# Two kept tiles of g for every unit, a ring of twelve, and a new slot layout in a sparse graph convolution

## The chip, the cores and the metric

One Trainium2 chip; the kernel uses one of its cores. The time is device microseconds of one execution, the median over several runs. Before the change: 1553.8 us, median of 3 runs (1552.07 to 1555.2). One execution was also profiled; it took 1553.88 us, of which the profile's span covers 1552.2 us.

## The reference

```python
HW = einsum('bnf,fo->bno', x, W)               # 8 x 4096 x 256, W is 256 x 256
A_norm = relu((A + A.T) * 0.5)                 # 4096 x 4096
D = sum(A_norm, axis=1)
d = D ** -0.5                                  # 0 where D is 0
out = relu(einsum('nm,bmo->bno', eye - d[:,None] * A_norm * d[None,:], HW))
y = layernorm(x + out, axis=-1)
```

A is an adjacency matrix with weights of 0.05 to 0.12. An entry (i, j) is there with a chance that falls with i and with j, so the first rows and columns (the hubs) are dense and the rest is sparse. The diagonal is always there. Everything is float32.

## The kernel before, in words

**First stage, to about 594 us.** A is symmetrised in 512 x 512 blocks and written to a DRAM tensor `a_dram`; the degrees give r = D^-0.5. In the same time g = r * (x W) is formed in row tiles of 128 x 2048 (8 batches times 256 outputs) and written to `g_dram`, 8192 bytes a row. The product of row tile 0 of the output, which is dense, is done there too (`lead`, L536).

**Second stage, from 594 us.** The other 31 row tiles are taken in 16 units: unit u holds row tiles 2u+1 and 2u+2, the last unit only one. The units run in the order `SEQ` (L24): 1 to 7, 0, 8 to 15. For a unit the kernel finds, on the chip, which rows of g it needs at all: those whose 256 columns of A_norm hold something. The first `HUBS[u]` row tiles of g are left out of this search: they are kept in SBUF over the whole stage (`hubs`, L865, loaded at L957), and are multiplied whole. All other rows are gathered.

A needed row is sorted by the 32-column strips that it touches. A row that touches one strip of the eight is of one of eight single kinds, and there are kinds of two strips, of one whole row tile, and one kind 0 for everything else (`KINDS`, L22). Each unit has a number of slots of 64 rows for each kind (`CAPS`), and the slots stand in an order (`FIRST`); two slots make a gathered tile of 128 rows. A row for which its kind has no slot left moves on to a wider kind, at last to kind 0. If kind 0 is full, a flag (`over`, L356) makes the kernel do all again densely at the end (L1211).

**The steps.** `steps_of` (L789) makes the list of TensorE steps of a unit, when the program is built, from CAPS, FIRST and HUBS alone. A whole step multiplies one tile (a kept hub or a gathered tile) with all 128 columns of one row tile: 4 banks of 512 columns. A round (L812) packs up to eight small products of 64 rows by 32 columns that lie on different parts of the array, taken from the first `REACH` = 5 tiles that still have some to do; it also goes over 4 banks. A float32 product is two instructions in the profile, so a whole step is 8 instructions on L1121 and a round of eight products 64.

**The ring.** Gathered tiles go into a ring of `RING` = 11 tiles (`gather`, L907). Each tile is two indirect DMAs on POOL's queue: L914 brings the weights from `a_dram` (128 x 128, or 128 x 256 for tiles that serve both row tiles), L922 the rows of g (128 x 2048; empty slots are skipped once the ring has been filled). `gather_ahead` (L932) is called after every step. Its rule is

```python
while eaten < asked and not uses_left[order[eaten]]:
    eaten += 1
while asked < len(order) and asked - eaten < RING:
    gather(asked)
    asked += 1
```

so slots come free in the order of asking: a tile still in use holds back all later ones.

**What else runs beside the steps.** The loop at L1131 places everything at a counted distance from the steps: `run_later(2)` after each step counts down what `after(n, ...)` has put off, so n is twice the number of steps. For each row tile there are the residual's load on ACT's queue (L725), the eviction on ACT (L731), the normalisation on VectorE (L741 to L774), and the store on SP's queue (L784), nine steps later. For each unit VectorE and TensorE make the index lists of a unit two to four places later (`prepare`, `lists`, L1049 and L1064). The rows of A for a hub are loaded on POOL (`load_hub_rows`, L895), 64 KB for each hub and row tile. An SP instruction after each bank of a round (L1188) keeps two rounds from writing one bank at a time.

Of the kernel before, what the change touches and what calls it, by code (L numbers as in the profile page):

```python
# [22 lines left out]

SEQ = [1, 2, 3, 4, 5, 6, 7, 0, *range(8, 16)]  # L24

HUBS = [2, 2, 2, 2, 3, 3, 2, 3, 3, 2, 3, 2, 3, 2, 3, 0]

CAPS = [
    [3, 4, 3, 3, 3, 2, 3, 3, 2, 3, 3, 3, 3, 3, 11],
    [3, 3, 3, 3, 3, 3, 3, 2, 3, 3, 2, 2, 2, 2, 6],  # L30
    [2, 3, 3, 3, 3, 3, 3, 3, 3, 2, 2, 2, 2, 2, 4],
    [3, 2, 3, 3, 2, 2, 2, 3, 3, 2, 2, 2, 2, 2, 3],
    [2, 2, 2, 3, 3, 3, 3, 3, 3, 2, 2, 2, 1, 1, 2],
    [2, 3, 3, 3, 3, 2, 3, 3, 3, 2, 1, 1, 1, 1, 2],
    [2, 2, 3, 3, 3, 2, 3, 3, 3, 2, 1, 1, 1, 1, 2],
    [2, 3, 3, 3, 3, 3, 3, 2, 2, 2, 1, 1, 1, 1, 1],
    [2, 2, 2, 3, 3, 2, 2, 3, 2, 2, 1, 1, 1, 1, 1],
    [2, 2, 2, 3, 3, 2, 2, 3, 3, 2, 1, 1, 1, 1, 1],
    [1, 3, 2, 3, 3, 2, 2, 3, 3, 1, 1, 1, 1, 1, 1],
    [1, 2, 3, 3, 3, 3, 3, 3, 3, 1, 1, 1, 1, 1, 1],  # L40
    [2, 2, 2, 2, 2, 2, 2, 2, 3, 1, 1, 1, 1, 1, 1],
    [2, 2, 2, 2, 2, 2, 2, 2, 2, 2, 1, 1, 1, 1, 1],
    [2, 2, 2, 2, 2, 2, 2, 2, 2, 1, 0, 0, 1, 1, 2],
    [3, 4, 4, 4, 4, 0, 0, 0, 0, 0, 0, 0, 0, 0, 0],
]

FIRST = [
    [0, 6, 10, 3, 13, 25, 19, 16, 27, 22, 44, 30, 47, 50, 33],
    [9, 0, 3, 6, 12, 18, 21, 16, 27, 24, 32, 30, 40, 42, 34],
    [3, 0, 5, 11, 8, 25, 19, 16, 22, 14, 34, 32, 38, 36, 28],  # L50
    [7, 2, 4, 10, 0, 24, 17, 19, 14, 22, 33, 26, 28, 35, 30],
    [0, 7, 5, 2, 9, 12, 23, 17, 20, 15, 31, 29, 26, 33, 27],
    [6, 8, 11, 0, 3, 22, 14, 17, 24, 20, 28, 33, 31, 32, 29],
    [0, 5, 7, 10, 2, 14, 16, 19, 24, 22, 32, 31, 33, 30, 28],
    [9, 6, 3, 0, 11, 17, 14, 22, 20, 24, 26, 28, 29, 30, 27],
    [2, 0, 10, 7, 4, 12, 19, 16, 21, 14, 24, 26, 28, 25, 27],
    [3, 10, 8, 5, 0, 22, 20, 12, 15, 18, 24, 26, 27, 28, 25],
    [0, 4, 7, 1, 9, 21, 19, 12, 16, 15, 26, 28, 24, 25, 27],
    [0, 10, 7, 1, 4, 15, 18, 12, 21, 24, 26, 28, 27, 30, 29],
    [0, 6, 8, 2, 4, 14, 10, 12, 16, 19, 24, 22, 20, 23, 21],  # L60
    [8, 2, 6, 4, 0, 10, 12, 14, 18, 16, 20, 22, 23, 24, 21],
    [0, 2, 4, 6, 8, 10, 12, 14, 16, 18, 20, 20, 20, 21, 22],
    [12, 15, 4, 0, 8, 20, 20, 20, 20, 20, 20, 20, 20, 20, 20],
]


# [1 line left out]
def kernel(  # L68
# [38 lines left out]
    QU = P // E  # L107
    NE = 2 * QU
    HOLD = 10
    RING = 11  # L110
    REACH = 5
    LATE = 18
    EPS = 1e-5
# [100 lines left out]
    def patterns(u):  # L214

        def t(shape, name, dtype=F32, **kw):
            return ipool.tile(shape, dtype, tag=name, name=f"{name}_{u}", **kw)
# [13 lines left out]
        nc.vector.tensor_tensor(diag, diag, own[:, :, :nb], ALU.max)  # L231
        if HUBS[u]:
            nc.vector.memset(used[:, :, : HUBS[u]], 0.0)
        several = t([P, NB], "several", bufs=1)
# [554 lines left out]
    def steps_of(u):  # L789
# [35 lines left out]
        def full(t, b):  # L825
            return [(t, None, b, None)]
# [9 lines left out]

        held = range(HUBS[u])
        out = [full(-1, 0)] if HUBS[u] else []
        starts = [full(t, 0) for t in whole[15]]
# [3 lines left out]
        if blocks(u) == 1:  # L843
            return out + [full(t, 0) for t in whole[0]]
        out += [full(-1, 1)] if HUBS[u] else []
        rows = [[full(t, 0), full(t, 1)] for t in whole[0]]
# [9 lines left out]
    with (  # L856
# [5 lines left out]
            gath.enter_context(tc.tile_pool(name=f"gath_{k}", bufs=1)).tile([P, G], F32, name=f"g{k}")  # L862
            for k in range(RING)
        ]
        hubs = [  # L865
            gath.enter_context(tc.tile_pool(name=f"hub_{h}", bufs=1)).tile([P, G], F32, name=f"g_hub{h}")
            for h in range(max(HUBS))
        ]
        ring_rows = [apool.tile([P, 2 * P], F32, tag=f"a{k}", name=f"ga{k}") for k in range(RING)]
        hub_rows = [  # L870
# [36 lines left out]
        def gather(n):  # L907

            u, t = order[n]
            both = t >= bounds[u][1]  # L910
            at, gt = ring_rows[n % RING], ring[n % RING]
            gi, ai = plan[u]
            with queue("pool"):
                nc.gpsimd.indirect_dma_start(  # L914
                    out=at if both else at[:, :P],
                    out_offset=None,
                    in_=a_pairs if both else a_rows,
                    in_offset=bass.IndirectOffsetOnAxis(ap=ai[:, t : t + 1], axis=0),
                    element_offset=P if both else 0,
                )  # L920
            with queue("pool"):
                nc.gpsimd.indirect_dma_start(  # L922
                    out=gt,
                    out_offset=None,
                    in_=g_dram,
                    in_offset=bass.IndirectOffsetOnAxis(ap=gi[:, t : t + 1], axis=0),
                    bounds_check=N if n < RING else N - 1,
                    oob_is_err=False,
                )
            got[u, t] = (at, gt, P if both else 0)  # L930

        def gather_ahead():  # L932
            nonlocal asked, eaten
# [4 lines that stand above are left out]
# [329 lines left out]
```

## Time and profile before

| what | value |
|---|---|
| time, median of 3 runs | 1553.8 us |
| profiled execution: time, and its span | 1553.88 us, 1552.2 us |
| first step of unit 1; first step of unit 15; last record of unit 15 | 594.2; 1504.4; 1525.5 us |
| busy: PE, DVE, POOL, ACT | 1428.7, 1040.1, 744.4, 364.0 us |
| DMA: moved, mean rate | 546.70 MB, 352 GB/s |
| q0 (POOL), q1 (SP), q10 (ACT): share of the 16 engines' span | 48.0%, 23.7%, 22.4% |

A line of groups gives the line, the engine, the operation, output<-input, the count, the busy time, the mean ns of one, and the idle time before it with what ended it. A line of waits says who waited for whom, for how long in total, how often, and the longest. A line of stretches gives the stretch, its length, then each engine's busy time with its number of instructions, the granted clock of TensorE, the mean busy share of the 16 DMA engines, and what they moved in GB/s. A line of the timeline has start, duration, engine, line, operation and, in brackets, the idle time before it and what ended that.

### The profile page before, as it was taken

Reading aid. Unit: us, or ns where it says so; the run is one execution under the profiler, and the core shown is the slowest. Engines: PE = TensorE matmul, PEld = TensorE weight load, DVE = VectorE, ACT = ScalarE, POOL = GpSimd, SP = SyncE. Lnnn points to the kernel's source line nnn. Section 1 sums busy time; section 2 is a strip of 40 time slices with the busy share of each in tenths; the row PEclk is TensorE's granted clock in tenths of the full one; section 3 lists DMA queues with packets and bytes.
Section 4 is the critical chain, followed back from the end, with each engine's and each line's share of the span. In section 5 each row is a group of like instructions: output and inputs, shape, how many; then the busy total and the mean of one; then the engine's idle time right before and its main releaser. Section 6 shows DMA issues by size and latency. Waiting matters only on the chain.

```text
span 1552.2 us, 29354 instructions
## 1 busy us (share of the span) xinstructions
PE 1428.7 (92%) x11008; PEld 766.6 (49%) x11008; DVE 1040.1 (67%) x3135; ACT 364.0 (23%) x462; POOL 744.4 (48%) x1271
## 2 busy tenths in 40 slices
PE   6999989898989987999999999799999898999992
PEld 5877867677867742333333433243343333334331
DVE  6676589979855645038659579499119978968554
ACT  3555544444544430010100100100010010011111
POOL 4012010011314226756675775767555776667751
PEclk9999999989999987999999999899999999999996
DMA  9999999999989998999998998999877999999994
GB/s 349 362 366 401 398 374 344 369 329 350 362 320 343 341 391 307 377 374 334 394 377 302 401 366 309 394 348 372 357 273 256 391 376 324 330 399 400 390 390 149
DMA packets 217749, 546.70 MB, mean 352 GB/s; under 512 B 19627, under 2 KB 107995, under 8 KB 183547
## 3 DMA queue, kind: packets, MB, share of 16 engines
q0 software_dynamic: 55216, 286.49, 48.0%
q1 hardware_dynamic: 93472, 126.89, 23.7%
q10 hardware_dynamic: 68912, 131.37, 22.4%
q8 instruction: 89, 1.46, 0.4%
q14 instruction: 60, 0.49, 0.1%
HBM read 442.89 MB, written 136.34 MB: 373 GB/s over the span
## 4 chain that ended last, share of the span: by engine, by line
PE 61%; DMA 16%; DVE 13%; issue 5%; POOL 3%; ACT 1%; SPq 0%; ACTq 0%; POOLq 0%; DVEq 0%
PE py L1121 40%; PE pg L578 9%; DMA g<-g_dram,gi 5%; PE lead L536 5%; DVE sym L472 4%; DMA out_dram<-xr 3%; PE xtr L567 3%; PE tr L468 3%; DMA xin<-in_x_dram 3%; DVE sums L479 3%; DMA a_dram<-sym 2%; POOL ga L914 1%; DMA ga<-a_dram,ai 1%; DMA xr<-in_x_dram 1%; ACT sym L476 1%
## 5 line engine op out<-in xcount | busy, mean ns | idle before, releaser
L1121 PE MATMUL py<-g,ga 64*32 64x512 f32 (+1 forms) x7024 | 614.6, 608 | 40.9 <-DMA g<-g_dram,gi 37.8
L1121 PEld LDWEIGHTS py<-g,ga 64*32 64x32 f32 (+1 forms) x7024 | 219.6, 112 | 420.7 <-issue 331.4
L914 POOL DMA_INDIRECT ga<-a_dram,ai x264 | 284.7, 1079 | 160.4 <-PE py L1121 86.2
L922 POOL DMA_INDIRECT g<-g_dram,gi x264 | 296.6, 1123 | 105.7 <-issue 64.0
L731 ACT ACTIVATE y<-py,minus_r 128x512 f32<-128x512 f32 x120 | 75.6, 687 | 836.1 <-PE py L1121 694.0
L1121 PE MATMUL py<-g_hub,gh 128*128 128x512 f32 x592 | 267.4, 599 | 1.7 <-DVE pos_k L210 1.7
L578 PE MATMUL pg<-w_sb,xt 128*128 128x256 f32 x1024 | 231.3, 384 | 5.8 <-ACT xt L568 4.0
L472 DVE TENSOR_TENSOR sym<-tr,adj 128x512 f32<-128x512 f32 x256 | 161.7, 682 | 78.0 <-PE tr L468 71.6
L578 PEld LDWEIGHTS pg<-w_sb,xt 128*128 128x128 f32 x1024 | 195.1, 193 | 34.1 <-ACT xt L568 4.4
L480 POOL TENSOR_SCALAR uses<-sums 128x64 uint8<-128x64 f32 x64 | 27.6, 431 | 350.6 <-DVE sums L479 312.2
L1121 PEld LDWEIGHTS py<-g_hub,gh 128*128 128x128 f32 x592 | 109.3, 190 | 154.8 <-issue 146.1
L479 DVE TENSOR_REDUCE sums<-sym 128x64 f32<-128x2048 f32 x64 | 145.4, 2278 | 54.4 <-ACT sym L476 54.4
L413 DVE COPY low<-lists 128x17 f32<-128x17 f32 (+7 forms) x14 | 2.4, 173 | 247.4 <-PE lists L401 247.4
L468 PE MATMUL tr<-ident,adj 128*128 128x128 f32 x1024 | 138.9, 285 | 29.8 <-DVE sym L472 16.9
L476 ACT ACTIVATE sym<-sym 128x2048 f32<-128x2048 f32 x64 | 122.8, 1918 | 126.5 <-DVE sym L472 126.5
L468 PEld LDWEIGHTS tr<-ident,adj 128*128 128x128 f32 x1024 | 118.4, 146 | 57.1 <-DVE sym L472 32.0
L741 DVE TENSOR_TENSOR xr<-xr,y 128x2048 f32<-128x2048 f32 x31 | 70.9, 2286 | 59.1 <-ACT y L731 29.3
L750 DVE BATCH_NORM_STATS2 stats<-xr 128x6 f32<-128x256 f32 x256 | 87.0, 412 | 1.1
L567 PE MATMUL xtr<-ident,xin 128*128 128x128 f32 x512 | 73.4, 294 | 14.5 <-DVE sym L472 12.8
L774 DVE TENSOR_SCALAR xr<-xr,mv,root 128x256 f32<-128x256 f32 x248 | 84.4, 411 | 0.6
L536 PE MATMUL lead<-gt,strip 128*128 128x512 f32 x176 | 83.5, 598 | 0.0
L568 ACT COPY xt<-xtr 128x512 f32<-128x512 f32 x128 | 67.8, 593 | 46.0 <-PE xtr L567 27.6
(152 smaller groups left out, 1041.3 us busy)
## 6 DMA issues: line engine op xcount, KB each, us to landing
adj<-in_adj_dram SPq DMA_DIRECT2D x64, 1024.0 KB, 10.2
a_dram<-sym ACTq DMA_DIRECT2D x64, 1024.0 KB, 9.9
out_dram<-xr SPq DMA_DIRECT2D x31, 1024.0 KB, 22.9
xr<-in_x_dram ACTq DMA_DIRECT2D x29, 1024.0 KB, 16.2
xin<-in_x_dram SPq DMA_DIRECT2D x44, 512.0 KB, 12.1
g_dram<-gt ACTq DMA_DIRECT2D x22, 1024.0 KB, 8.0
xin<-in_x_dram POOLq DMA_DIRECT2D x20, 512.0 KB
g_dram<-held ACTq DMA_DIRECT2D x10, 1024.0 KB, 11.9
```

The costliest lines, as they stand in the source:

```text
L468: ins = nc.tensor.transpose(pt[:, c * P : (c + 1) * P], tji[:, c, a * P : (a + 1) * P], ident)
L472: nc.vector.tensor_add(sym[:, a, :], pt, tij[:, a, :])
L476: nc.scalar.activation(sym, sym, AF.Relu, scale=0.5)
L479: nc.vector.tensor_reduce(sums, sym.rearrange("p a (c q) -> p a c q", q=E), AX.X, ALU.add)
L536: nc.tensor.matmul(lead[c], lhsT=strip, rhs=g[:, c * S : (c + 1) * S], start=not done, stop=len(done) == NB - 1, skip_group_check=True,)
L567: nc.tensor.transpose(pt[:, k, c, :], xin[b // H][:, b % H + k, c * P : (c + 1) * P], ident)
L578: ins = nc.tensor.matmul(pg[:, k * FO : (k + 1) * FO], lhsT=xt[:, b + k, c, :], rhs=w_sb[:, c, :], start=(c == 0), stop=(c == FC - 1),)
L750: nc.vector.bn_stats(stats[:, b, :], z[:, b, :])
L774: nc.vector.tensor_scalar(z[:, b, :], z[:, b, :], mv[:, b, 0:1], rstd[:, b : b + 1], ALU.subtract, ALU.mult,)
L914: nc.gpsimd.indirect_dma_start(out=at if both else at[:, :P], out_offset=None, in_=a_pairs if both else a_rows, in_offset=bass.IndirectOff ...
L922: nc.gpsimd.indirect_dma_start(out=gt, out_offset=None, in_=g_dram, in_offset=bass.IndirectOffsetOnAxis(ap=gi[:, t : t + 1], axis=0), boun ...
L1121: return nc.tensor.matmul(py[2 * u + 1 + b][c][cols, :], lhsT=at[ps, off + cols.start : off + cols.stop], rhs=gt[ps, c * S : (c + 1) * S], ...
```

## The change

All numbers in it are tables and one constant; no line of the program's logic differs. `HUBS` has 2 for every unit but the last (seven units had 3), so the third kept tile of g and its rows of A are gone. `RING` is 12. `CAPS` and `FIRST` are new.

```diff
-HUBS = [2, 2, 2, 2, 3, 3, 2, 3, 3, 2, 3, 2, 3, 2, 3, 0]
+HUBS = [*[2] * 15, 0]
 CAPS = [
     [3, 4, 3, 3, 3, 2, 3, 3, 2, 3, 3, 3, 3, 3, 11],
-    [3, 3, 3, 3, 3, 3, 3, 2, 3, 3, 2, 2, 2, 2, 6],
-    [2, 3, 3, 3, 3, 3, 3, 3, 3, 2, 2, 2, 2, 2, 4],
+    [3, 3, 3, 3, 3, 3, 3, 2, 2, 2, 2, 2, 3, 3, 6],
+    [3, 3, 3, 3, 2, 2, 2, 2, 3, 3, 2, 2, 2, 2, 4],
...
 FIRST = [
-    [0, 6, 10, 3, 13, 25, 19, 16, 27, 22, 44, 30, 47, 50, 33],
-    [9, 0, 3, 6, 12, 18, 21, 16, 27, 24, 32, 30, 40, 42, 34],
+    [9, 12, 0, 6, 3, 19, 16, 21, 24, 26, 44, 30, 47, 50, 33],
+    [12, 0, 3, 9, 6, 21, 18, 24, 16, 26, 28, 30, 41, 32, 35],
...
     HOLD = 10
-    RING = 11
+    RING = 12
```

What `steps_of` makes of the tables, before > after, and the rows that a unit gathers (counted on the reference's inputs by the kernel's rule: a row outside the kept tiles with an entry in the unit's columns):

| unit (in order) | steps | gathered tiles | rows gathered |
|---|---|---|---|
| 1 | 21 > 21 | 22 > 22 | 2599 |
| 2 | 18 > 18 | 20 > 19 | 2325 |
| 3 | 17 > 17 | 19 > 19 | 2128 |
| 4 | 16 > 15 | 17 > 18 | 1943 > 2046 |
| 5 | 16 > 15 | 17 > 17 | 1874 > 1972 |
| 6 | 14 > 14 | 17 > 17 | 1855 |
| 7 | 14 > 13 | 16 > 16 | 1773 > 1874 |
| 0 | 28 > 28 | 27 > 27 | 3000 |
| 8 | 14 > 12 | 15 > 17 | 1690 > 1778 |
| 9 | 12 > 12 | 15 > 16 | 1652 |
| 10 | 13 > 12 | 15 > 14 | 1584 > 1680 |
| 11 | 12 > 12 | 16 > 15 | 1594 |
| 12 | 13 > 11 | 13 > 15 | 1489 > 1569 |
| 13 | 11 > 11 | 13 > 13 | 1537 |
| 14 | 13 > 11 | 12 > 13 | 1429 > 1505 |
| 15 | 5 > 5 | 10 > 10 | 987 |
| sum | 237 > 227 | 264 > 268 | 29459 > 30101 |

Of the steps, 121 > 114 are whole and 116 > 113 are rounds. Of the tiles, 64 > 68 bring weights for both row tiles. In every unit kind 0 has room for the rows that come to it, before and after, so the dense fallback is not run. SBUF holds the same 14 tiles of 128 x 2048: 11 + 3 before, 12 + 2 after, and since the ring is laid out ahead of the hubs, its twelfth tile lies where hub 0 lay, and hubs 0 and 1 where hubs 1 and 2 lay.

## The prediction

> **What bounds the kernel now.** I read the page first: which engine and which queue is full.
>
> ```profile
> PE 1428.7 (92%) x11008; PEld 766.6 (49%) x11008; DVE 1040.1 (67%) x3135; ACT 364.0 (23%) x462; POOL 744.4 (48%) x1271
> ...
> DMA  9999999999989998999998998999877999999994
> ...
> q0 software_dynamic: 55216, 286.49, 48.0%
> q1 hardware_dynamic: 93472, 126.89, 23.7%
> q10 hardware_dynamic: 68912, 131.37, 22.4%
> ...
> PE py L1121 40%; PE pg L578 9%; DMA g<-g_dram,gi 5%; PE lead L536 5%; DVE sym L472 4%; DMA out_dram<-xr 3%; PE xtr L567 3%; PE tr L468 3%; DMA xin<-in_x_dram 3%; DVE sums L479 3%; DMA a_dram<-sym 2%; POOL ga L914 1%; DMA ga<-a_dram,ai 1%; DMA xr<-in_x_dram 1%; ACT sym L476 1%
> ```
>
> Two resources are nearly full at once: TensorE at 92%, and the DMA engines, whose three queues add up to 94.1%. So time saved on one of them counts only as far as the other allows. The change touches only the second stage (594.2 to 1525.5 us), so next I cut that into stretches, and looked within them for places where the DMA engines stand still.
>
> ```profile
> 689.40:1050.80 361.40, 349.71 (x3353) 137.54 (x3352) 271.97 (x1006) 30.67 (x49) 246.61 (x235) 0.98 0.96 356
> 1050.80:1159.80 109.00, 105.73 (x862) 39.32 (x861) 41.33 (x165) 4.85 (x8) 65.31 (x66) 0.97 0.90 344
> 1159.80:1504.40 344.60, 329.03 (x3099) 130.14 (x3098) 270.25 (x993) 34.99 (x57) 235.99 (x224) 0.98 0.95 357
> ...
> 690.00:730.00 40.00, 40.00 (x409) 14.94 (x415) 38.05 (x146) 2.42 (x4) 25.78 (x25) 1.00 0.87 305
> 830.00:850.00 20.00, 16.38 (x160) 5.98 (x162) 18.77 (x88) 0.00 (x0) 10.32 (x11) 0.95 0.67 234
> 950.00:970.00 20.00, 20.00 (x125) 7.52 (x124) 19.08 (x60) 0.00 (x0) 10.33 (x9) 1.00 0.69 228
> 1150.00:1190.00 40.00, 40.00 (x333) 16.68 (x333) 31.43 (x134) 4.37 (x7) 17.36 (x17) 1.00 0.60 208
> ```
>
> The first three are units 2 to 7, unit 0, units 8 to 14. The others are holes in the DMA: 5.2, 6.6, 6.2 and 16.0 us of nothing moving (length times one minus the DMA share). With 1.6 at 1020, 7.8 at 1120, 1.6 at 1240, 3.3 at 1280 and 3.8 at 1330, from the same view, the holes are 52 us. What makes them is seen on POOL and PE beside one of them:
>
> ```profile
> 833.48 0.58 POOL L902 DMA_DIRECT2D gh<-a_dram  x1 [1.72 <-PE py L1121]
> 836.92 0.55 POOL L902 DMA_DIRECT2D gh<-a_dram  x1 [2.85 <-PE py L1121]
> 840.44 0.98 POOL L914 DMA_INDIRECT ga<-a_dram,ai  x1 [2.97 <-PE py L1121]
> 841.73 1.04 POOL L922 DMA_INDIRECT g<-g_dram,gi  x1 [0.30 <-issue]
> ...
> 848.10 7.45 PE L1121 MATMUL py<-g,ga 64*32 64x512 f32 x94 [3.62 <-DMA g<-g_dram,gi]
> ...
> POOL ga L914 <- PE py L1121: 86.2, 77, 9.7
> PE py L1121 <- DMA g<-g_dram,gi: 37.8, 18, 6.5
> ```
>
> The ring is full, so POOL asks for no tile until TensorE has finished with the oldest (840.44). Then several are asked for at once, and TensorE itself waits for the one it needs next (to 848.10). Each hole in the DMA is paid back later as a TensorE wait.
>
> **What the Trainium skill says.** "DMA: Bandwidth & Descriptors", section "Issuing engines are not separate DMA queues": transfers issued by different engines run on the same 16 DMA engines and interleave. The trace agrees: the shares of three queues sum to 94.1%. The same page, "Anatomy of one DMA — SWDGE (gpsimd) path", puts a fixed 2 us on such a transfer; here a tile asked for at 841.73 freed TensorE at 848.10, 6.4 us, with others beside it. "Perfetto Trace Analysis", "Identifying the Most-Contended Engine": the same gap repeating on the engine that should be full can mean too few buffers for the next tile. The nine holes, with POOL waiting for TensorE, fit that.
>
> **The sum of the stage before.** I take step times from the starts of consecutive steps: a whole step is 3.53 us (two of them on a hub tile fill 7.03 us at 829.59), a full round 3.43 to 3.59. The index-list products stretch 14 steps by 1.24. So 237 x 3.53 + 14 x 1.24 = 854 of the 930.7 us between 594.2 and the last step's end at 1524.9; 77 us are waits, 19 of them at the first two steps, for the ring's first tiles.
>
> **The change, part by part.**
>
> *Steps on TensorE.* 237 to 227: 10 x 3.53 = 35.3 us less. If its waits stayed at 77 us the kernel would take 1518.6. They can't, since the DMA gets more to do.
>
> *Bytes.* 642 more gathered rows of 8192 bytes: +5.26 MB. One hub tile fewer: -1.05 MB. 14 fewer loads of 64 KB for the hubs' rows of A: -0.92 MB. Four more tiles, as four more of 128 KB: +0.52 MB. Sum +3.81 MB. POOL's queue moved 286.49 MB in 48.0% of 1552.2 us, 2.60 us per MB, so +9.9 us of DMA time. Nothing hides it where the engines are full, so it counts whole; were all of it to fall into holes, it would be nothing. I take 9.9. POOL's own issue work, 0.95 + 0.30 + 1.00 + 0.30 = 2.55 us a tile at its usual pace, grows by 10 us for four tiles and falls by 14 x 0.6 = 8.
>
> *The twelfth ring tile.* Before each hole one more tile can be asked for. A tile is on average 30101 / 268 = 112 rows, 0.92 MB, and 0.08 MB of weights: 2.6 us of transfer. A hole shrinks by that, or by its own size if less; the two at 1120 and 1150 lie in one stretch paced by TensorE (unit 0 and the start of 8), and gain once. So 6 x 2.6 + 2 x 1.6 = 18.8 us. Bounds: 0, if something else holds the asking back, and 18.8.
>
> *The new layout.* Fewer steps also bring the release of the oldest tile forward: one step fewer in units 4, 5, 7 and 10, two in 8, 12 and 14. What is left of the holes near these is 4.0 (830), 3.6 (950), 13 (1150). One step of 3.5 in the first two and two in the third could take up to 14 us; a layout that keeps a tile longer would take 0. To choose I walked the steps by the ring's rule and counted, for each tile, the steps between being asked for and first needed. Before, 39 tiles have four steps or fewer and 9 have two or fewer; after (with ring 12), 11 and 1. Stretches of two or more steps in which nothing is asked for: 32 before, 20 after. That says the layout doesn't undo the ring's gain, but the count includes the ring's part, so I take 5 of the 14.
>
> *The start.* The first gather was asked for at 593.33, behind three hub loads; now behind two. Hub 0 lies where hub 1 lay, whose load waited for `lead` until 587.78 and not 584.58. That is covered: TensorE is in `lead` until 594.18 and the load needs some 4 us. Uncovered it would cost up to 3.2. The 2.7 us of the missing hub are in the byte sum.
>
> *What stays.* Unit 0 has the same 28 steps (99 us of TensorE for 82 of transfers), unit 15 the same 5, and after the last step the same finish: 1524.9 to 1552.2.
>
> Sum: +9.9 - 18.8 - 5 = -13.9 us on the profiled execution's 1553.88, so **1540.0 us**. That execution lies 0.1 us from the median of the runs shown, so no correction is made. In TensorE's ledger: 818.7 us busy and about 98 us waiting, 21 more than before.
>
> **Rivals.**
>
> *The holes don't close, only the bytes count (slower).* Place: units 4 to 14. POOL needs 2.55 us to ask for a tile, the engines 2.6 us to bring it; after a drought POOL asks for six in a row, slowed to 1.9 us a piece when the queue is full, so an extra slot need not fill a hole. Then +9.9: 1563.8. It decides once the holes shrink by less than 9.9 of their 52 us. For it: POOL is as slow as the DMA. Against: at the start of a hole POOL is idle and waits for TensorE, 86.2 us in 77 waits. Between this and my case lies a partial gain. Chance 0.13 for ending slower.
>
> *VectorE becomes the bound.* In units 2 to 7 it is busy 271.97 / 6 = 45.3 us a unit. A unit of 12 steps is 12 x 3.53 + 1.24 = 43.6 us, and units 8 to 11 now have 12 each while index lists are still made. A unit's first step must wait till VectorE has read the counts: unit 12 shows 1.7 us of it (DVE pos_k L210). Four units at 1.7 give 7 us back: 1547. Against: transfers need about 51 us a unit there (unit 9: 13.5 MB of g and 1.3 MB of weights at 2.60, and four row tiles of 1.05 MB at the 2.90 us per MB of q1), more than VectorE's 45.3. Chance 0.15.
>
> *It does what the step count says.* TensorE bound, waits unchanged: 1518.6. It would need the DMA engines to do 9.9 us more in 35 less, that is nearly all of the 52 us of holes closed, though unit 0 alone keeps most of 24. Chance 0.04 for under 1528.
>
> *No change.* The gains and the bytes cancel, within 3 us (0.2%, about what a measurement of this kernel can tell from none): 0.05.
>
> **How the numbers follow.** The likeliest case, holes closing by 19 to 29 us, has 0.63: its own range is 1533 to 1547 and the forecast 1540. With VectorE (0.15) and the step count (0.04), and a rest of 0.82 between them, faster is 0.82, same 0.05, slower 0.13. The range for 8 in 10 reaches from 1530 (the byte cost at nothing for half, and most of the 14 us of the layout) to 1553 (gain and bytes all but cancel); about 0.06 lie below and 0.14 above.
>
> **What would show it.** On L1121 the hub matmuls fall from 592 to 480, those on gathered tiles go from 7024 to 7136 (838 small products and 54 whole steps, 8 each); L914 and L922 rise to 268, L902 falls to 60. Right: the DMA share of units 2 to 7 and 8 to 14 rises, the holes near 830 and 950 shrink to under 4 us, POOL's wait for PE falls well under 86 us, and PE's wait for g rises. Units 2 to 7 end some 8 us earlier than at 1050.8. Wrong: holes of the same size at new places, or PE's waits named DVE at the start of units 9 to 12.

## The result, and the profile after

The changed kernel takes 1529.47 us (median of 4 runs, 1526.87 to 1530.94) against 1554.5 us (1552.07 to 1556.66) for the kernel before. The ratio is 0.9838, with a 95% interval of 0.9817 to 0.9858: 25 us faster, where 13.9 were forecast. The direction was right. The time lies half a microsecond below the range of 1530 to 1553.

The profiled execution took 1529.14 us, of which 1527.3 are the span. The page of the changed kernel, the same lines as before:

```profile
PE 1390.9 (91%) x11008; PEld 753.8 (49%) x11008; DVE 1040.8 (68%) x3135; ACT 363.7 (24%) x462; POOL 739.9 (48%) x1264
...
DMA  9999999999989997998999999999978999999994
...
q0 software_dynamic: 55392, 290.44, 48.7%
q1 hardware_dynamic: 93472, 126.89, 24.2%
q10 hardware_dynamic: 68912, 131.37, 22.8%
...
PE py L1121 31%; DMA g<-g_dram,gi 9%; PE pg L578 9%; PE lead L536 5%; DMA a_dram<-sym 4%; DVE sym L472 3%; DMA out_dram<-xr 3%; PE tr L468 3%; DMA xin<-in_x_dram 3%; PE xtr L567 3%; DVE sums L479 2%; DMA ga<-a_dram,ai 2%; POOL ga L914 2%; DMA adj<-in_adj_dram 1%; DVE stats L750 1%
```

TensorE loses 37.8 us of busy time, close to the 35.3 of the ten steps. POOL's queue moved 3.95 MB more, yet the three queues together are busy for no longer: 95.7% of 1527.3 is 1461.6 us, where before 94.1% of 1552.2 was 1460.6. On the chain, the steps' share falls from 40% to 31% and the gathered tiles' transfers rise from 5% to 9%.

The stretches of the changed kernel: units 2 to 7, unit 0, units 8 to 14, then units 2 to 14 as one, and the places of two of the old holes (the second lies in unit 6, which now starts at 927.1 us and not at 937.2, so its place is ten us earlier).

```profile
688.00:1033.00 345.00, 336.73 (x3124) 131.59 (x3123) 270.58 (x1004) 30.04 (x48) 238.98 (x228) 1.00 0.98 374
1033.00:1145.30 112.30, 105.79 (x858) 39.67 (x857) 43.52 (x167) 5.17 (x8) 65.69 (x67) 0.95 0.91 348
1145.30:1474.70 329.40, 304.94 (x3195) 121.38 (x3194) 269.84 (x992) 34.89 (x56) 235.20 (x222) 0.97 0.99 373
687.90:1474.70 786.80, 747.56 (x7175) 292.71 (x7174) 584.03 (x2161) 70.09 (x112) 539.87 (x516) 0.98 0.97 370
830.00:850.00 20.00, 20.00 (x177) 7.44 (x184) 18.77 (x92) 0.00 (x0) 10.55 (x12) 1.00 0.92 330
940.00:960.00 20.00, 20.00 (x180) 7.24 (x164) 18.74 (x88) 0.00 (x0) 13.84 (x16) 1.00 0.90 339
```

Units 2 to 14 of the kernel before, in the same view:

```profile
689.40:1504.40 815.00, 784.47 (x7311) 307.01 (x7310) 583.55 (x2162) 70.52 (x113) 547.91 (x524) 0.98 0.94 355
```

The DMA share is rounded to a hundredth; summed over the packets of the trace, the DMA engines were busy for 770.0 us of these units and idle for 45.0 before, and busy for 765.0 and idle for 21.8 after. So 23 us of holes closed. The busy part fell a little, although the bytes in it rose: 355 GB/s over 815.0 us is 289 MB, 370 over 786.8 is 291 MB. The gain lies on both sides of unit 0. By step starts, units 2 to 7 took 361.4 us and take 344.0, units 8 to 14 took 344.6 and take 329.4. Unit 0 itself takes 4.4 us longer (109.0 and 113.4; it starts at 1031.9, a little before the 1033.00 of the stretch shown). Unit 15, which was to stay as it was, takes 26.2 us and not 21.1: TensorE stands still there for 3.9 us before a tile of g, where it stood 1.4.

Waits between 590 and 1505 us in the changed kernel (who waited for whom: total, times, longest):

```profile
ACT y L731 <- DMA out_dram<-xr: 71.3, 2, 40.6
POOL ga L914 <- PE py L1121: 69.8, 76, 7.1
...
PE py L1121 <- DMA g<-g_dram,gi: 34.3, 16, 5.0
...
PE lists L401 <- ACT y L731: 6.5, 1, 6.5
...
PE py L1121 <- DVE pos_k L210: 5.0, 3, 2.0
```

POOL waits 69.8 us for TensorE where it waited 86.2, and TensorE waits 34.3 us for g where it waited 37.8. By step starts, the stage (first step to the end of the last) fell from 931.3 to 907.3 us. With 227 steps of 3.53 us and 14 x 1.24 for the index lists, 88.7 us of it are beyond the bare steps, against 77.3 before.

Not all of this is waiting. TensorE stands still for 55.0 us of the stage, against 43.6 before; in the other 34 us, before and after, steps took longer than 3.53. Part of that is the granted clock. A line of the timeline and one of a stretch in it (TensorE alone), then the same form of product within that stretch and, for comparison, between 1340 and 1361 us at full clock (count, busy us, mean ns):

```profile
1369.15 8.79 PE L1121 MATMUL py<-g,ga 64*32 64x512 f32 x124 [2.61 <-DMA g<-g_dram,gi]
1369.70:1373.10 3.40, 3.40 (x46) 0.51 0.97 362
L1121 PE MATMUL py<-g,ga 64*32 64x512 f32 x40 | 4.4, 955 | 0.0
...
L1121 PE MATMUL py<-g,ga 64*32 64x512 f32 x120 | 7.3, 592 | 0.0
```

In the stage of the changed kernel the clock was granted at half in eight stretches of 3.4 to 17.1 us, 54.6 us in all, in which TensorE was busy for 39 us; before in six, 51.2 us in all and 33 busy. Each of the fourteen starts within 5 us after the beginning of a standstill of 2.0 to 6.5 us. So in these two traces a wait of TensorE often costs more than its own length. As an estimate, half of the 39 and 33 us, 20 and 17 us of the stage, are lost in this way.

The standstills that have grown are not those for g: TensorE waits for VectorE at the start of a unit (1.7 to 5.0 us), and once 6.5 us for an eviction on ACT (1.1 before).

### The profile page after: what moved, and what is told of

Its sections match the earlier page's. It is cut to its first block, busy times and chain, and to the rows that moved or that the text cites. A ratio compares the mean times of both kernels' runs of the same rounds, so it can differ in the third digit from the quotient of the medians.

```text
span 1527.3 us, 29344 instructions
## 1 busy us (share of the span) xinstructions
PE 1390.9 (91%) x11008; PEld 753.8 (49%) x11008; DVE 1040.8 (68%) x3135; ACT 363.7 (24%) x462; POOL 739.9 (48%) x1264
## 4 chain that ended last, share of the span: by engine, by line
PE 50%; DMA 23%; DVE 16%; issue 6%; POOL 3%; ACT 2%; SPq 0%; ACTq 0%; POOLq 0%; DVEq 0%
PE py L1121 31%; DMA g<-g_dram,gi 9%; PE pg L578 9%; PE lead L536 5%; DMA a_dram<-sym 4%; DVE sym L472 3%; DMA out_dram<-xr 3%; PE tr L468 3%; DMA xin<-in_x_dram 3%; PE xtr L567 3%; DVE sums L479 2%; DMA ga<-a_dram,ai 2%; POOL ga L914 2%; DMA adj<-in_adj_dram 1%; DVE stats L750 1%
## 5 line engine op out<-in xcount | busy, mean ns | idle before, releaser
L1121 PE MATMUL py<-g,ga 64*32 64x512 f32 (+1 forms) x7136 | 627.0, 608 | 41.3 <-DMA g<-g_dram,gi 34.3
L1121 PEld LDWEIGHTS py<-g,ga 64*32 64x32 f32 (+1 forms) x7136 | 229.2, 113 | 422.8 <-issue 333.8
L914 POOL DMA_INDIRECT ga<-a_dram,ai x268 | 285.6, 1066 | 139.7 <-PE py L1121 69.8
L1121 PE MATMUL py<-g_hub,gh 128*128 128x512 f32 x480 | 220.7, 601 | 5.0 <-DVE pos_k L210 5.0
L1121 PEld LDWEIGHTS py<-g_hub,gh 128*128 128x128 f32 x480 | 87.6, 190 | 132.7 <-issue 118.2
L380 DVE TENSOR_TENSOR hot<-iota_q,at 128x1024 bf16<-128x1024 f32 x64 | 74.4, 1217 | 7.2 <-DMA a_dram<-sym 7.2
## 6 DMA issues: line engine op xcount, KB each, us to landing
xr<-in_x_dram ACTq DMA_DIRECT2D x29, 1024.0 KB, 20.4
xin<-in_x_dram SPq DMA_DIRECT2D x44, 512.0 KB, 12.6
```

The source lines that it names most:

```text
L914: nc.gpsimd.indirect_dma_start(out=at if both else at[:, :P], out_offset=None, in_=a_pairs if both else a_rows, in_offset=bass.IndirectOff ...
L1121: return nc.tensor.matmul(py[2 * u + 1 + b][c][cols, :], lhsT=at[ps, off + cols.start : off + cols.stop], rhs=gt[ps, c * S : (c + 1) * S], ...
```

## The experiments

Two theories stood at the start. By the prediction's, the ring's twelfth tile closes the holes (18.8 us) and the bytes cost 2.60 us per MB. By another, the tables do it: fewer steps and another layout, with bytes that cost little where another engine sets the pace. A gain or loss in us below is the difference of two ratios times 1554; it lies within 2 us of the difference of the medians. The interval of one ratio reaches some 3 to 4 us to either side, so a difference of two kernels under about 5 us is not clear of its uncertainty.

### The ring alone, and the tables alone

The changed kernel with eleven ring tiles:

```diff
-    RING = 12
+    RING = 11
```

> The changed kernel with the ring back at 11 tiles; tables and hubs as changed. The sum of the prediction has 18.8 us for the twelfth tile: about 1548 us. If the missing 10 us came from the new tables and the fewer steps instead, the ring is worth less than was said and this stays near 1537 to 1542. If the ring gave more than 18.8, over 1550.

Measured: 1530.75 us, ratio 0.9851 (0.9825 to 0.9877). The twelfth tile is worth 2 us on top of the new tables, within what these runs can tell from nothing.

Next, only the seven units that lose their third hub get new rows of `CAPS` and `FIRST` (4, 5, 7, 8, 10, 12, 14); the other nine (the expectation below says eight) keep the old ones. Two hubs for all. One kernel has eleven ring tiles, the other twelve.

```diff
-HUBS = [2, 2, 2, 2, 3, 3, 2, 3, 3, 2, 3, 2, 3, 2, 3, 0]
+HUBS = [*[2] * 15, 0]
 CAPS = [
     [3, 4, 3, 3, 3, 2, 3, 3, 2, 3, 3, 3, 3, 3, 11],
     [3, 3, 3, 3, 3, 3, 3, 2, 3, 3, 2, 2, 2, 2, 6],
...
```

> Ring 11, two hubs everywhere, the new CAPS and FIRST only in the seven units that lost a hub; the other units have the old ones. So it holds all ten removed steps and most of the bytes, but neither the ring nor the new layout elsewhere. By the prediction's price of bytes (+9.9 less some 4 for steps): about 1560. If the bytes cost next to nothing and the ten steps count: 1535 to 1545.

> As the one before, with ring 12. Against the changed kernel only the layout of the eight units with unchanged hubs is undone. Walking the steps by the ring's rule, tiles with a lead of four steps or fewer are 19 here and 11 in the changed kernel (39 before). If leads as short as this are what makes the waits, some 3 to 6 us slower than the changed kernel, 1533 to 1536; if the layout of these units is worth nothing, 1529.

Measured: 1534.79 us with eleven tiles, ratio 0.9881 (0.9862 to 0.9899); 1526.6 with twelve, 0.9827 (0.9804 to 0.985). So most of the gain, 18.5 us, is there without a twelfth tile and without a new layout of the other nine units. A twelfth tile on top of this is worth 8.4 us, and the new layout of the nine other units nothing that shows (the whole change is at 0.9838), though it has fewer tiles with a short lead, 11 and not 19. No run has a twelfth tile with the old tables. Units 2 to 14 of the two kernels with eleven tiles, the mixed one first:

```profile
687.30:1482.30 795.00, 754.83 (x7216) 295.21 (x7215) 583.16 (x2160) 70.08 (x112) 554.26 (x521) 0.98 0.98 369
```

```profile
684.70:1477.80 793.10, 752.09 (x7176) 295.93 (x7175) 584.99 (x2161) 70.07 (x112) 553.23 (x520) 0.98 0.98 369
```

The DMA share is 0.98 in both, with the old ring: 18.4 and 19.1 us idle by the packets, against 45.0 before and 21.8 with twelve tiles. So the holes close without the twelfth tile. Nor are holes the same as time: with eleven tiles on the new tables the stretch is 6.3 us longer than with twelve, at less idle DMA, since the engines are busy for 774.0 us with the same tables' rows and not for 765.0. The page "Perfetto Trace Analysis" of the Trainium skill ("Optimization Strategy"), which the prediction followed, says that such gaps can mean too few buffers; here the step from eleven to twelve gave 2 to 8 us, not 19.

### What a megabyte costs

Both kernels with the gathered rows of the highest indices left out, so that 12.6 MB less is fetched in each. The steps stay as they are, and the output lacks these rows' part (the stale contents of the ring are multiplied in their place).

```diff
-    bounds_check=N if n < RING else N - 1,
+    bounds_check=N if n < RING else N - 257,
```

> The changed kernel, but the gather of g (L922) skips rows 3840 and above in every tile after the ring's first lap: some 1500 rows of 8 KB, 12.3 MB, are left out, with every instruction kept (it computes without these rows' products). If bytes cost what the prediction said, 2.60 us per MB: 32 us faster, 1497. If TensorE waits because tiles are asked for late, and not because the engines are full: no more than 5 to 12 us faster, 1517 to 1525.

> The kernel before, with the same rows left out of the gathers as in the changed kernel: some 1500 rows of g, 12.3 MB, with every instruction kept. In the changed kernel that gave about 7 us, 0.6 us per MB and not 2.60. If bytes count as little here, 4 to 9 us faster, 1545 to 1550. If the kernel before was held by the transfers and only the changed one is not: 20 to 32 us, 1522 to 1534.

Measured: 1522.26 us for the changed kernel, ratio 0.9795 (0.9763 to 0.9827), 6.7 us less than with all rows; 1545.8 for the one before, 0.9942 (0.9925 to 0.9959), 9.0 us less. That is 0.53 and 0.71 us per MB, and about 1.0 and 0.9 at the far end of the uncertainty. The prediction charged 2.60. Where the rest went is in the stretch over units 2 to 14 of the changed kernel with fewer rows:

```profile
685.80:1469.60 783.80, 746.33 (x7175) 295.06 (x7174) 586.06 (x2163) 70.50 (x113) 551.86 (x518) 0.98 0.96 359
```

Against 786.8 us at 0.97 and 370 GB/s, the engines move 10 MB less (359 x 783.8 is 281 MB; 370 x 786.8 is 291) and the stretch is 3 us shorter. By the packets, the engines are busy for 748.8 us and not 765.0, and idle for 35.1 and not 21.8. So 16 us of transfers were taken out, less than the 26 that 2.60 us per MB would give, and 13 of the 16 became idle DMA and not time. A share of 95% did not mean that the next byte costs a full share.

### What a step costs

The ten removed steps are put back into the changed kernel, with the same gathers. In the units that lost steps, hub 1 is multiplied once or twice more, so its part of the output is counted more than once.

```diff
+        held = [*held, *[1] * {4: 1, 5: 1, 7: 1, 8: 2, 10: 1, 12: 2, 14: 2}.get(u, 0)]
...
-        out += weave(rounds[:first_b1], [full(-1 - h, 0) for h in held[1:]], starts)
+        out += weave(rounds[:first_b1], [full(-1 - h, 0) for h in held[1:3]], starts)
...
-            [full(-1 - h, 1) for h in held[1:]],
+            [full(-1 - h, 1) for h in [1, *held[3:]] if HUBS[u]],
```

> The changed kernel, but the product of hub 1 is done once more in units 4, 5, 7 and 10 and twice more in 8, 12 and 14 (hub 1 counts double there): 237 steps as before, no byte and no gather more. If the removed steps are what made the kernel faster, some 19 us (what the mixed kernel with ring 11 gained) come back: 1545 to 1552. If the DMA engines set the pace, as the prediction had it, the steps fill waits and it stays under 1537.

Measured: 1595.51 us, ratio 1.0271 (1.0247 to 1.0294). This run doesn't measure steps. After the first product with hub 1, the next unit's rows of A were loaded into the same buffer, and the second product waited for that load, which the waits of this kernel name:

```profile
PE py L1122 <- DMA gh<-a_dram: 69.2, 8, 15.4
```

So the rows for the next unit were then loaded after the last use only:

```diff
-                if t < 0:
+                if t < 0 and not any((u, s) in steps[q + 1 : q + 40] for s in [step]):
```

> The experiment with the steps put back, mended: the earlier one loaded the next unit's rows of A over those that the doubled product still had to read, so that product waited for a load (77 us of TensorE waiting for gh<-a_dram) and its time says nothing on steps. Now the load follows the last use. 237 steps, the same bytes and gathers as the changed kernel (hub 1 counts double in seven units). If the removed steps made the kernel faster: 1543 to 1552. If transfers set the pace: under 1537.

Measured: 1533.83 us, ratio 0.9869 (0.9842 to 0.9896), 4.8 us above the changed kernel (the two intervals still overlap by a little). The prediction's third rival, that the step count sets the time, is refuted: this kernel has the 237 steps of the kernel before and is 20.4 us faster than it. The same count as above gives 57.5 us beyond the bare steps instead of 88.7, so thirty-one of the thirty-five microseconds of extra steps don't show in the stage. Eighteen of them go into standstills of TensorE (36.7 us instead of 55.0; for g 23.0 instead of 34.3, and the 6.5 for ACT are gone). The other thirteen come back because the steps take less long: the clock is at half for 30.7 us of the stage instead of 54.6, which by the same estimate (half of TensorE's busy time there, 21.7 us instead of 39.2) makes nine of the thirteen.

The other way, ten steps more are left out: the first product with hub 1, in all units but 1 to 5 (and the last, which has none), so that part of the output is missing. Nine loads of 64 KB fall away with them.

```diff
+        held = [h for h in held if not (h == 1 and u not in (1, 2, 3, 4, 5))]
```

> The changed kernel with the first product of hub 1 left out in the ten units from 6 on (one step of 3.53 us fewer in each, 35 us of TensorE; these products are missing from the result; nine loads of 64 KB fewer). If steps still count as ten of them did in the change (some 19 us for ten): 1508 to 1515. If units of 10 and 11 steps are too short for what runs at a counted distance beside them (stores, residual loads, lists) or for the transfers: within 8 us of the changed kernel, or slower.

Measured: 1520.75 us, ratio 0.9788 (0.9759 to 0.9817), 7.8 us less. A further step is worth 0.8 us of its 3.5: of the 35.3 us, 13.0 become standstill (68.0 us instead of 55.0), and 12.5 are lost because the other steps take longer, with the clock at half for 75.1 us of the stage instead of 54.6 (nine or ten of the 12.5 by the same estimate).

### VectorE as the bound

The changed kernel normalises one of the eight batches; the other seven are stored without their normalisation. That takes 71 us from VectorE.

```diff
-        for b in range(B):
+        for b in range(1):
```

> The changed kernel, but seven of the eight normalising instructions of a row tile (L774) are left out, except in the last one: 2.3 us less of VectorE for each of 31 row tiles, 71 us in all (those seven batches come out as x plus the product, not normalised). If VectorE were the bound of the 11 and 12 step units: 10 us or more faster, and the waits for DVE pos_k (5.0 us in 3) gone. If it only has that wait: 3 to 6 us. If TensorE or transfers set the pace everywhere: under 3 us.

Measured: 1522.1 us, ratio 0.9789 (0.9772 to 0.9806), 7.6 us less. VectorE is in the path, but no more than the others: 71 us less of it, 12.6 MB less for the DMA engines, or ten steps less of TensorE each give 7 to 8 us.

### The new wait on ACT

At unit 13 ACT stands still for 40.6 us before an eviction, and TensorE's list product waits 6.5 us for that eviction. ACT's own timeline in the changed kernel, then TensorE's:

```profile
1409.25 19.93 ACTq L725 DMA_DIRECT2D xr<-in_x_dram  x2
1429.28 2.42 ACT L731 ACTIVATE y<-py,minus_r 128x512 f32<-128x512 f32 x4 [40.55 <-DMA out_dram<-xr]
```

```profile
1430.02 1.00 PE L401 MATMUL lists<-val,hot 128*128 128x20 bf16 x32 [6.46 <-ACT y L731]
```

The residual's load (L725) goes into a buffer that an earlier store must have left. That load stands on ACT's queue and the eviction behind it. It may be that with shorter units a store that is put off nine steps comes later against the next load. If so, an earlier store should help. `LATE` is counted in half steps:

```diff
-    LATE = 18
+    LATE = 14
```

> The changed kernel with LATE = 14, stores two steps earlier than with 18. With 8 the stores stood on SP's queue waiting for VectorE (266 us), the bank turns queued behind them, and TensorE waited 181 us for SP. If VectorE is behind by two or three steps only now and then, the stores free the residuals' buffers 7 us earlier and the wait on ACT's queue at unit 13 shrinks: 1521 to 1527. If VectorE is behind by more than that in most units: slower, 1535 to 1560.

and the same with 8:

> The changed kernel with LATE = 8: a row tile is stored four steps after its normalisation and not nine. In the changed kernel the residual loads of unit 13 wait on ACT's queue for stores to free their buffers, and the evictions queue behind them (71 us of ACT waiting for out_dram<-xr in 2 waits, 6.5 us of the lists' products waiting for ACT), which no trace of before shows. If this is a new wait that the shorter units brought, some 5 to 10 us faster: 1520 to 1525, with that wait gone. If the wait is hidden, or the earlier stores hold back the gathers: 1529 or more.

Measured: 1575.21 us with 14, ratio 1.0143 (1.0117 to 1.0169); 1665.91 with 8, ratio 1.0724 (1.0701 to 1.0746). Both are far slower. The store is now issued before VectorE has finished, so SP stands at it. Two answers of the waits of the kernel with 8, SP's own and TensorE's:

```profile
SPq L784 <- DVE xr L774: 266.5, 20, 23.4
```

```profile
PE py L1121 <- SPq L1188: 180.8, 13, 19.7
```

In the changed kernel these are 13.8 and 3.5 us. Behind the store on SP stand the instructions that give the banks free between rounds (L1188), and TensorE waits for those. So the delay that makes the one wait on ACT keeps a much larger one off SP; whether that one wait costs the kernel anything was not settled, since no run takes it away alone.

### The start of the stage

With eleven ring tiles and two hubs, POOL's first requests come earlier than with twelve. POOL's timeline of the changed kernel, then of the changed kernel with eleven tiles:

```profile
587.41 0.55 POOL L957 DMA_DIRECT2D g_hub<-g_dram  x1 [16.43 <-PE lead L536]
588.09 1.08 POOL L902 DMA_DIRECT2D gh<-a_dram  x2
590.84 0.53 POOL L957 DMA_DIRECT2D g_hub<-g_dram  x1 [1.67 <-issue]
591.36 1.06 POOL L902 DMA_DIRECT2D gh<-a_dram  x2
592.72 1.05 POOL L914 DMA_INDIRECT ga<-a_dram,ai  x1 [0.30 <-issue]
```

```profile
586.29 0.55 POOL L957 DMA_DIRECT2D g_hub<-g_dram  x1 [13.42 <-PE lead L536]
...
591.37 1.05 POOL L914 DMA_INDIRECT ga<-a_dram,ai  x1 [0.30 <-issue]
```

The hubs lie where the `lead` product works until the first stage ends, and the gathers stand behind them on POOL. The experiment lays the hubs out ahead of the ring, which itself moves on by two tiles (three in the kernel before); no other line changes:

```diff
+        hubs = [...]
         ring = [...]
-        hubs = [...]
```

> The changed kernel with the hubs laid out ahead of the ring. With ring 12 the hubs lie one place further on, their loads wait for a later product of lead, and POOL's gathers queue behind them: the first gather is asked for 1.0 us before lead's end, as in the kernel before, and not 4.7 us before it as with ring 11 and two hubs. If that is what the twelfth tile cost at the start: the first gather 4 us or more earlier against lead's end, and the kernel 3 to 8 us faster, 1521 to 1527. If the first gathers then wait for places of their own, or the gain is lost in later waits: 1528 to 1531.

> The changed kernel with ring 11 and the hubs laid out ahead of the ring. Against the same with ring 12 (1519.4 us) it gives the worth of the twelfth tile without what it cost at the start. In the trace of ring 11 the first two steps waited 13.4 us and in that of ring 12 19.0, so of the 1.3 us measured some 5.6 were lost there: theory, ring 12 is worth about 7 and this runs at 1524 to 1529. If the twelfth tile is worth nothing by itself: 1518 to 1521. If the prediction's 18.8 holds and something else hid it: 1536 or more.

> The kernel before with the hubs laid out ahead of the ring and nothing else changed. In the changed kernel this gave 10 us. If the start's wait is passed on whole whatever the tables: 8 to 12 us faster, 1542 to 1546. If in the kernel before the time is given back at later waits, where the ring of 11 runs dry: under 5 us, 1549 to 1554.

Measured: 1519.41 us for the changed kernel so laid out, ratio 0.9785 (0.9759 to 0.981), 8.2 us less; 1521.05 with eleven tiles, 0.9794 (0.9778 to 0.9811); 1547.52 for the kernel before, 0.9966 (0.9952 to 0.9979), 5.3 us less. POOL's timeline of the first of these:

```profile
572.02 0.55 POOL L957 DMA_DIRECT2D g_hub<-g_dram  x1 [3.01 <-DMA g_dram<-held]
...
576.70 1.05 POOL L914 DMA_INDIRECT ga<-a_dram,ai  x1 [1.49 <-DMA a_dram<-diag]
```

The first gather is asked for 16 us earlier, at 576.70 and not at 592.72, and no longer behind a wait for `lead`. By step starts, unit 1's time beyond its bare steps falls from 19.0 to 6.9 us (it was 19.9 in the kernel before), and the stretch at half clock there from 17.1 to 3.4 us. Even with the start out of the way the twelfth tile is worth only 1.4 us (1521.05 to 1519.41) on the new tables.

Together with the mixed tables and twelve tiles, where the layout is worth 11.2 us:

> The mixed kernel with ring 12 (1526.6 us, 2.9 less than the changed kernel, within what was measured as uncertain) with the hubs laid out first: a candidate for the fastest. If the 10 us of the start and the 2.9 of the older layout add up: 1514 to 1518. If the layout's difference was chance: 1518 to 1521.

Measured: 1515.16 us, ratio 0.9755 (0.9732 to 0.9778). It is the fastest of all, 38 us below the kernel before and 13 below the change.

### What the third hub cost

What is left is to split the 18.5 us of the mixed tables with eleven tiles. First, the 1.05 MB load of a third hub is put back into that kernel, with its buffer (the same edit in the loop that makes the buffers and in the one that loads them); nothing uses it.

```diff
-        for h in range(max(HUBS)):
+        for h in range(3):
```

> The mixed kernel with ring 11 (1534.8 us), but the third hub is still loaded at the start, 1 MB ahead of the first gathers, and never used. It tells how much of the 18.5 us that the mixed kernel gained is the missing load at the start. First gather 3.7 us later against lead's end than in the mixed kernel, and 3 to 6 us slower: 1538 to 1541. If the start doesn't matter: 1535. If it is most of the gain: over 1545.

Measured: 1537.68 us, ratio 0.9903 (0.9885 to 0.9922), 3.4 us more, though the intervals overlap.

Then two kernels were to show the rest: the same load and the ten steps put back as above; and the old hubs in the steps, with the rows of the third hub gathered as well, so that they are multiplied twice.

> The mixed kernel with ring 11 and the third hub's load put back (1537.7 us), and the ten steps put back by doubling products of hub 1, with no byte more: 237 steps. In the changed kernel ten steps cost 4.8 us. If a step costs the same here: 1541 to 1545, and some 8 us of the mixed kernel's gain are due to the tables and to the 14 loads on POOL. If the ring of 11 makes steps dearer: 1548 or more, and nothing is left for the tables.

> The mixed kernel with ring 11, with all the third hub's work put back in its seven units: 14 steps, 14 loads of 64 KB on POOL and the 1 MB at the start, 241 steps in all, while the tables still gather the third hub's rows too (these count double). If the third hub's own work is what the mixed kernel got rid of: all of its 18.5 us come back and some more, 1551 to 1558. If the new tables of the seven units are themselves better for the waits: 1540 to 1548.

Measured: 1790.83 us, ratio 0.9971 (0.9954 to 0.9989), and 1804.12, ratio 1.0047 (1.0031 to 1.0062). These two ran on a chip on which the kernel before takes 1796.07 us (35 runs), and not 1552 to 1555 as in every other comparison. There, the waits of the first of them are led by one line:

```profile
PE py L1122 <- SPq L1189: 181.7, 81, 7.5
```

This is TensorE waiting for SP's turn of a bank (one line lower, since a line was added), 0.2 us in the profile of the kernel before and 3.5 us in the changed one. With another bound, the ratios can't be set against the rest, and the split stays open.

## Why the prediction was wrong

**Two terms of the sum failed, and their errors partly cancelled.** The first is the bytes: "Nothing hides it where the engines are full, so it counts whole", +9.9 us. At the measured 0.53 to 0.71 us per MB, 3.81 MB would cost 2.0 to 2.7 us (an estimate: these figures come from rows taken out of all units, not put in where the change put them), so the term was 7 to 8 us too dear. The reasoning behind it took the queue's busy time over its bytes for a fixed price. But the engines' busy time isn't fixed by the bytes: over units 2 to 14 it is 770.0 us for 289.1 MB before and 765.0 us for 291.2 MB after, summed over the packets, and the mean packet of 8 KB took 333 ns before and 328 after. And most of what is taken out leaves idle engines, not time.

The second is the twelfth ring tile, -18.8 us. On the new tables it measured 2.0 us, within the uncertainty of nothing; 1.4 with the hubs first, and 8.4 on the mixed tables. The tables do what it was to do: with eleven tiles the changed kernel is already 23 us faster, where the terms without the tile (+9.9 - 5) make it 5 us slower.

With the byte term alone put right, the sum is -21 to -21.8 us and the time 1532 to 1533, some 3 us from the measured one. That closeness is luck, since 18.8 us of it still stand for the wrong cause.

**The holes were right in size by chance.** Forecast: holes shrink by 18.8 (twelfth tile) and 5 (layout), 23.8 in all; measured, 23.2 us less idle DMA in units 2 to 14, and the holes at 830 and 950 are 20 x 0.08 = 1.6 and 20 x 0.10 = 2.0 us, under the 4 forecast. But with eleven tiles the idle DMA had fallen by 26 to 27 us already.

**Fewer steps and the layout:** 5 us forecast; the steps alone measured 4.8, which is not clear of its uncertainty, and the mixed tables as a whole 18.5. In TensorE's ledger, 88.7 us beyond the bare steps stand against a forecast of 98. The prediction called all of it waiting; 55.0 us are.

**The start** was called covered. The load of hub 0 was covered; the gathers that stand behind it on POOL were not. With eleven tiles and two hubs the first gather is asked for 4.5 us ahead of TensorE's first step (591.37 and 595.89), with twelve 0.9 us (592.72 and 593.58), as in the kernel before (593.33 and 594.18). By step starts, unit 1 takes 13.4 us beyond its bare steps with eleven and 19.0 with twelve. So the earlier start that two hubs give with eleven tiles is gone again with the twelfth, which moves the hubs on by one place. Against the kernel before nothing was lost (19.9 us), which is why the error did not show in the total.

**The signs.** The counts came out as forecast: 480 hub matmuls, 7136 on gathered tiles, 268 gathers and 60 loads of hub rows. The DMA share rose on both sides of unit 0, and POOL's wait for TensorE fell, by 16 us. Two signs were wrong: TensorE's wait for g was to rise and fell by 3.5 us, and units 2 to 7 ended 19 us earlier (1050.8 to 1031.9), not 8. Both fit bytes that cost less than charged.

**The rivals.** "Only the bytes count" (0.13) and "no change" (0.05) are refuted by the time itself. VectorE as the bound (0.15) has a true core, with 5.0 us of waits at unit starts against 1.7, and 7.6 us for 71 us less work; these waits grew by 3 us, not 7. The step count (0.04) is refuted by the ten steps put back.

**Still open:** of the 18.5 us of the mixed tables with eleven tiles, some 5 may go to the steps and about 3 to the third hub's load (neither clear of its uncertainty; the 5 were measured on the changed kernel). The other 10, and the 2 to 3 that the added bytes took, may lie in the fourteen fewer loads of hub rows on POOL, in fewer uses that hold a ring tile, or in the seven units' layout. For the first speaks that POOL stood before such loads, waiting for TensorE, for 20.0 us before (two of these waits are in the prediction's hole at 830) and for 10.0 after; no run tells the three apart.

## What to carry to other kernels

A busy share over the bytes moved is the average price of a byte, not the price of the next one: near 95%, take some bytes out and measure, before charging the average. When several engines hold each other up in turn, relieving any one may give only a small part of what it is relieved of (here 7 to 8 us for 35 to 71). When waits are counted as the stage's length less its bare steps, look at the granted clock too, since steps that run slower after a wait are counted with it. Before more buffers are put in for holes in the DMA, ask what else holds the asking back: here the same holes closed under other tables with the buffers as they were, and at the start it was the loads that stand ahead on the asking engine's queue.

## What the hardware showed that was not expected

- At a DMA share of 0.94 to 0.97, taking 12.6 MB out saved 0.5 to 0.7 us per MB, about a quarter of the 2.60 that share over bytes gives.
- Fewer steps on TensorE mean more waits, and more time at half clock after them: 30.7, 54.6 and 75.1 us of the stage with 237, 227 and 217 steps in otherwise like kernels.
- One constant of the store's delay moves the kernel by 46 us (14) and by 136 us (8), through stores on SP that stand before the turns of the banks.
- The order in which the hubs and the ring are laid out is worth 5 to 11 us in four kernels; in the changed one the first gather is asked for 16 us earlier.
- A chip on which the same program takes 1796 us and not 1554, with TensorE's waits for SP at 182 us in 81 waits in a kernel close to it. The profile doesn't show why SP's turn comes later there.
